# Block product 5 of the K and V projections by seven smaller products

## The chip, the cores and the metric

The kernel runs on one core of a Trainium2 chip. The metric is the device time of one execution in microseconds (us), taken as the median of several runs; lower is better. Engines are named as in the profile: PE is TensorE (matrix products), PEld its weight loads, DVE is VectorE, ACT is ScalarE, POOL is GpSimd, SP is SyncE, which here only issues DMAs.

## The reference

A cross-attention layer followed by a feed-forward layer, in float32. There are 8 batches of 128 queries and 128 keys, a width of 512, 32 heads of 128, and a feed-forward width of 1376.

```python
x = x + xattn(layernorm(x), ctx, mask)      # xattn adds its own residual, and has an RMS norm first
  h_q = rmsnorm(h) @ w_q.T ; h_k = ctx @ w_k.T ; h_v = ctx @ w_v.T      # 512 -> 32 heads x 128
  score = softmax(where(mask, h_q h_k^T + position_bias, -inf))
  out = (score @ h_v) @ w_out.T
x = x + (silu(x' @ Wg.T * ag) * (x' @ Wu.T * au)) @ Wd.T * ad           # x' = layernorm(x)
```

## The kernel before

**Seven products for eight.** Each large matrix product is cut into 2 x 2 blocks and computed with the seven products of Strassen's scheme in Winograd's form instead of eight. For a projection, the weights give the blocks a11, a12, a21, a22 and the sums s1, s2, s4 (`combine_rows`, `sums_a`, on GpSimd; a21 is overwritten), the context tokens give the other factor (`ctx_t`). Numbered 1 to 7 the products add up to four output parts: product 1 goes to all, 6 to all but (1,1), 7 to (2,2) and (2,1), 5 to (2,2) and (1,2), while 2, 3 and 4 go to one part each: (1,1), (1,2) and (2,1).

**Two levels.** Of the 14 key and value projections of groups 1 to 7 (a group is four heads), eleven are "parted": the values of group 1 (v1), and keys and values of groups 2 to 6 (k2 to v6). There, products 1, 6, 7 and 5 are made as large tiles (`four`: two tiles for each product, banks "mm", copied out by ACT in L379, product 5 added to its two parts by VectorE in L377). Products 2, 3 and 4, the block products with a single target, are each split once more into 2 x 2 blocks and made by seven smaller products (`inner`, `inner_T` for keys, `inner_V` for values). `inner` takes seven steps. A step multiplies one of the seven small products for all three blocks, into a pair of banks ("one" or "two"), and VectorE adds what comes out to the output (L401). The banks accumulate over the steps: small products 1, 6, 7, 4 use the pair "one" and 2, 5, 3 the pair "two", in the order 2, 1, 6, 7, 4, 5, 3.

The smaller products need sums of their own. `inner_rows` makes them of the weights on GpSimd: one set of four additions over blocks 2 and 4 together (256 elements each), one set over block 3 (128 elements). `inner_tokens` makes them once of the tokens: for blocks 2 and 3 at the start, for block 4 in four additions that `ctx_later` hands out to VectorE one by one, one for each of the batches 0 to 3 of group 0.

**The order of the work.** `later_kv` is a generator that emits a projection's large tiles and, behind them, single steps of the projection's `inner`, one tile and one step in turn; the last five steps lie among the tiles of the next projection. It also calls `begin` (the next projection's `combine_rows`) and `inner_rows` at certain tiles k. The attention runs over groups g and batches b: `probabilities` (scores `sc` in L512, added to the masked bias in L516, row maximum, four exponentials in L525, row sums in L532, division L536), `transpose_p` (a VectorE transpose L273, a DMA `turned` to memory and a DMA `pT` back, L275 and L280), and `attend` (`av`, L558), which runs three batches later. After each batch, products are drawn from `later_kv` until their units (`FULL` for a tile, `PART` for a step) reach `due(g, b)`; so the projections of group g+1 fill TensorE between the batches of group g.

Engines wrapped in `InOrder` keep the program's order: TensorE, VectorE and ACT up to batch 3 of group 0, GpSimd up to the end of group 1. Everything else is ordered ahead of time by the framework's planner, which goes by the order of the program and its own estimate of times, and may bring later work forward.

The pool `ipool` holds the token sums (one tile for each inner block) and the row sums; `spool` holds s1, s2, s4 and `wpool` the weights, with three buffers each.

Of the kernel before, what the change touches and what calls it, by code (L numbers as in the profile page):

```python
# [10 lines left out]
F32 = mybir.dt.float32  # L11
# [6 lines left out]
P = 128  # L18
# [16 lines left out]
class Later:  # L35
# [10 lines left out]
    def next(self, engine):  # L46
        if self.calls:
            op, args, kw = self.calls.pop(0)
            getattr(engine, op)(*args, **kw)
# [15 lines left out]
def xattn_ffn_kernel(  # L65
# [32 lines left out]
    HC = DC // 2  # L98
    HW = GW // 2
# [15 lines left out]
    proj, rows, attn, wts = ExitStack(), ExitStack(), ExitStack(), ExitStack()  # L115
# [183 lines left out]
    def sums_a(eng, a11, a12, a21, a22, s1, s2, s4):  # L299

        eng.tensor_tensor(s1, a21, a22, ADD)
        eng.tensor_tensor(s2, s1, a11, SUB)
        eng.tensor_tensor(a21, a11, a21, SUB)
        eng.tensor_tensor(s4, a12, s2, SUB)
        return {1: a11, 2: a12, 3: s4, 4: a22, 5: s1, 6: s2, 7: a21}
# [9 lines left out]
    def combine_rows(name, w):  # L315

        a11, a12 = w[:, :HC, :HW], w[:, HC:, :HW]
        a21, a22 = w[:, :HC, HW:], w[:, HC:, HW:]
        s = spool.tile([P, 3, HC, HW], F32, tag="S", name=f"S_{name}")
        s1, s2, s4 = s[:, 0], s[:, 1], s[:, 2]  # L320
        rows = sums_a(gpsimd, a11, a12, a21, a22, s1, s2, s4)
        rows["lower"] = w[:, HC:]
        return rows

    def token_sums(eng3, eng4, b11, b12, b21, b22, t1, t2, t4):
# [57 lines left out]


    SINGLE = (2, 3, 4)

    def inner(name, multiply, places, banks=None, order=(2, 1, 6, 7, 4, 5, 3)):

# [15 lines left out]
    def inner_T(name, a, b, heads):  # L404
# [8 lines left out]

        return inner(name, multiply, (((2, 3), upper), ((4,), lower)))

    def inner_V(name, a, b, pairs):
        def multiply(n, i, out, first):
            for k in range(2):
                kv_tensor.matmul(  # L419
                    out[:, bass.ts(k, S)], b[n][i][:, bass.ts(k, S)], a[n][i],  # L420
                    start=first and k == 0, stop=True, skip_group_check=True,
                )

        def left(r, c, m):
            to = pairs[c - 1].rearrange("p k (h n) -> p h k n", h=2)[:, :, :, bass.ts(r - 1, P)]
            return [(to, m.rearrange("p h (k n) -> p h k n", k=2))]

        def right(r, c, m):
            to = pairs[c + 1][:, :, bass.ts(r - 1, P)]
            return [(to, m[:, 0].rearrange("p (k n) -> p k n", k=2))]  # L430

        return inner(name, multiply, (((2, 4), left), ((3,), right)))

    def numbered(b11, b12, b21, b22, t1, t2, t3, t4):
        return {1: b11, 2: b21, 3: b22, 4: t4, 5: t1, 6: t2, 7: t3}
# [161 lines left out]

    FULL, PART, FIRST = 4, 3, 3.8  # L600

    def later_kv():


        def place(n):
            t = ipool.tile([P, 4, HW], F32, tag=f"t{n}", name=f"t_c{n}")
            return (t[:, k] for k in range(4))

        def inner_rows(name, w):

            s = ipool.tile([P, 3, 3, P], F32, tag="rows", name=f"s_{name}", bufs=2)
            lower = w["lower"].rearrange("p c (n r q) -> p c n r q", n=2, r=2)
            both = [lower[:, c, :, r] for r in range(2) for c in range(2)]
            three = [w[3][:, c, bass.ts(r, P)] for r in range(2) for c in range(2)]
            sums = sums_a(gpsimd, *both, *(s[:, k, :2] for k in range(3)))
            a = {n: {i: rows[:, k] for i, rows in sums.items()} for k, n in enumerate((2, 4))}
            a[3] = sums_a(gpsimd, *three, *(s[:, k, 2] for k in range(3)))
            return a

        todo = [(g, kind) for g in range(1, NG) for kind in "kv"]  # L620
        made, rows = {}, {}

        def begin(n):

            g, kind = todo[n]
            if g not in made:
                made[g] = dict(zip("kv", kv_w.pop(g)))
            rows[n] = combine_rows(f"{kind}{g}", made[g].pop(kind))

        begin(0)  # L630
        b, steps = inner_tokens(vector, ctx_t, HW, place, (2, 3)), iter(())
        b.update(inner_tokens(ctx_later, ctx_t, HW, place, (4,)))
        for n, (g, kind) in enumerate(todo):
            name, w = f"{kind}{g}", rows.pop(n)
            out = kvs.setdefault(g, ([], []))["kv".index(kind)]
            parted = 0 < n and g + 1 < NG
            if parted:
                blocks, smaller = (blocks_T, inner_T) if kind == "k" else (blocks_V, inner_V)
                tiles = four(name, *blocks(name, w, ctx_t, out))
            else:  # L640
                tiles = (project_T if kind == "k" else project_V)(name, w, ctx_t, out)
            for k in itertools.count():

                if k == 5 and n + 1 < len(todo):
                    begin(n + 1)
                if k == 2 and parted:
                    a = inner_rows(name, w)
                if next(tiles, "none") == "none":
                    break
                yield FULL if n else FIRST  # L650
                if k == 6 and parted:
                    steps = smaller(name, a, b, out)
                if next(steps, None):
                    yield PART

# [8 lines left out]
    kv_tensor = InOrder(tc, nc.tensor)  # L664
# [26 lines left out]
    for n, _ in enumerate(first_kv()):  # L691
        if n in moments_at:
            pair[moments_at[n]] = norm1_moments(moments_at[n])
        if n in scales_at:
            b = scales_at[n]
# [182 lines left out]
    def due(g, b):  # L878


        tiles, steps = 2 * 8 * FULL, 2 * 7 * PART
        late = 5 * PART
        if g == 0 and b < 4:
            return (5 + 3 * b) * FIRST
        if g < NG - 2:
            start = 14 * FULL if g == 0 else g * (tiles + steps) - late
            end, n, k = (g + 1) * (tiles + steps) - late, 4 if g == 0 else B, b - 4 if g == 0 else b
        else:
            start, n, k = g * (tiles + steps) - late, B, b
            end = start + late + 25 * FULL  # L890
        return start + (end - start) * (k + 1) / n - 1.5
# [5 lines left out]
    for g in range(NG):  # L897
# [21 lines left out]
        for b in range(B):  # L919
# [14 lines left out]
            if g == NG - 1:  # L934


                if b + 2 < B:
                    biased.append(masked_bias(gpsimd, g, b + 2, pb))
                for _ in range(2):
                    wo_later.next(gpsimd)  # L940
                if wo_sums:
                    wo_sums = wo_sums(gpsimd)

                def between():
                    if b == 0:
                        next(products)
                    fetched[b] = att_sums(b, 0, come.pop((b, 0)), vector)

                p = probabilities(g, b, qT, kT, pb, between, biased.pop(0))
            elif g == 0 and b < 4:  # L950
                def one():
                    nonlocal done
                    done += next(products)

                def one_and_sum():
                    ctx_later.next(vector)
                    one()

                if b == 0:
                    biased = [masked_bias(gpsimd, g, k, pb) for k in range(2)]  # L960
                biased.append(masked_bias(gpsimd, g, b + 2, pb))
                p = probabilities(g, b, qT, kT, pb, one_and_sum, biased.pop(0), one)
            elif g == 0 and b < 6:
                p = probabilities(g, b, qT, kT, pb, s=biased.pop(0))
            else:
                p = probabilities(g, b, qT, kT, pb)
                if g == NG - 2:
                    for _ in range((0, 1, 1, 1, 1, 2, 2, 2)[b]):
                        wo_later.next(InOrder(tc, nc.gpsimd))
# [299 lines left out]
    def inner_F(i, a, outs):  # L1269
        def multiply(n, k, out, first):  # L1270
            nc.tensor.matmul(  # L1271
                out, a[n][k], fine_t[n][k], start=first, stop=True, skip_group_check=True
            )


        def both(k, r, c, m):
            to = outs[k][r - 1].rearrange("p (c n) -> p c n", c=2)[:, :, bass.ts(c - 1, HW)]
            return to, m

        def upper(r, c, m):  # L1280
            return [both(0, r, c, m)]

        def lower(r, c, m):
            to, _ = both(0, r, c, m)
            return [both(1, r, c, m), (to[:, 1], m[:, 1])]

        pl = ps.pools[1]
        banks = [
            pl.tile([P, 2, HW], F32, tag=tag, name=f"i_{i}_{k}", bufs=bufs)
            for k, (tag, bufs) in enumerate(3 * [("m", 3)] + [("tp", 1)])  # L1290
        ]
        return inner(
            f"f{i}", multiply, (((2, 3), upper), ((4, 5), lower)), (banks[:2], banks[2:]),
            (2, 1, 5, 6, 3, 7, 4),
        )

    gpsimd = nc.gpsimd
# [203 lines left out]
```

## Time and profile before

| | us |
|---|---|
| median of 3 runs | 1074.88 (1074.33 to 1076.42) |
| the profiled execution | 1076.96 |
| its span | 1075.2 |
| mean granted TensorE clock | 0.998 of full |
| TensorE busy | 1066.8 |
| VectorE busy | 675.3 |
| GpSimd busy | 489.8 |
| ACT busy | 332.5 |

The profile is of one execution. Its time is 1.76 us longer than its span, and 2.08 us longer than the median of the runs. Attention of group 0 begins at about 242 us, group 0's batches end near 291 us, and each of the groups 1 to 5 then takes 60.3 us. The parted projections lie from 269 to 617 us. Lines are named L401 and so on; a line can be that of a helper (L60 is `InOrder`). In rows of groups, the name left of the arrow is what is written, then come partitions x elements, the count, the busy time in us, the mean of one in ns, and idle time of the engine before it.

### The profile page before, as it was taken

How to read it: one execution, taken by the hardware profiler on the slowest of the kernel's cores; microseconds unless marked ns; L12 is line 12 of the kernel's file. 1: busy time of each engine (PE TensorE's matmuls, PEld its weight loads, DVE VectorE, ACT ScalarE, POOL GpSimd, SP SyncE). 2: the span in 40 equal slices, each digit the busy share in tenths (PEclk: the TensorE clock that was granted, in tenths of full speed). 3: DMA queues.
4: the chain of work that ended last, by engine and by line, in shares of the span. 5: the costliest groups of instructions: out<-in, count | busy, mean ns of one | idle time of the engine just before them, and what ended most of it. 6: DMA issues, size and time to landing. Idle time of an engine off the chain costs nothing.

```text
span 1075.2 us, 14043 instructions
## 1 busy us (share of the span) xinstructions
PE 1066.8 (99%) x4904; PEld 811.3 (75%) x4904; DVE 675.3 (63%) x1232; ACT 332.5 (31%) x902; POOL 489.8 (46%) x543
## 2 busy tenths in 40 slices
PE   9999999999999999999999999999999999999998
PEld 5656666655878888887978769998888875666887
DVE  4653443447757777777777766894454338889852
ACT  2633323214444444444444334221000012333100
POOL 6233455525655455555553373662000337897010
PEclk9999999999999999999999999999999999999999
DMA  9613344545665455464555566873542532110011
GB/s 291 196 57 118 117 152 166 192 165 198 196 206 184 160 164 183 157 211 165 198 187 187 169 213 214 274 235 125 190 138 78 171 124 59 40 41 18 1 40 40
DMA packets 124693, 161.82 MB, mean 151 GB/s; under 512 B 15600, under 2 KB 77296, under 8 KB 124624
## 3 DMA queue, kind: packets, MB, share of 16 engines
q1 hardware_dynamic: 110208, 129.73, 36.5%
q10 hardware_dynamic: 12544, 24.38, 6.5%
q0 software_dynamic: 1872, 6.82, 2.0%
q8 instruction: 39, 0.64, 0.2%
q14 instruction: 30, 0.25, 0.1%
HBM read 104.81 MB, written 56.10 MB: 150 GB/s over the span
## 4 chain that ended last, share of the span: by engine, by line
PE 93%; DMA 3%; DVE 2%; ACT 1%; issue 1%; ACTq 0%; POOL 0%; SPq 0%; DVEq 0%; POOLq 0%
PE mm_q L458 10%; PE m L843 9%; PE mm_k L458 9%; PE mm_v L479 9%; PE m L60 7%; PE d L1407 6%; PE i_q L406 6%; PE i L1271 6%; PE i_v L419 5%; PE mm_f L1312 5%; PE i_k L406 4%; PE av L558 4%; PE sc L512 4%; PE mm_k L60 3%; PE mm_v L60 2%; PE mm_q L60 1%
## 5 line engine op out<-in xcount | busy, mean ns | idle before, releaser
L497 POOL TENSOR_TENSOR s<-pb,mneg 128x512 f32<-128x512 f32 x40 | 61.3, 1533 | 112.1 <-DVE p L536 86.3
L401 DVE TENSOR_TENSOR q<-q,i_q 128x512 f32<-128x512 f32 x98 | 49.9, 550 | 82.2 <-PE i_q L406 82.0
L525 ACT ACTIVATE s<-s,nmx 128x128 f32<-128x128 f32 x240 | 93.4, 390 | 23.3 <-DVE nmx L60 11.7
L563 ACT COPY aT<-av 128x512 f32<-128x512 f32 x60 | 35.1, 586 | 162.6 <-PE av L558 130.3
L60 POOL TENSOR_TENSOR s<-pb,mneg 128x512 f32<-128x512 f32 x24 | 36.7, 1533 | 79.2 <-DVE p L60 39.6
L379 ACT COPY q<-mm_q 128x512 f32<-128x512 f32 x56 | 31.5, 588 | 94.9 <-PE mm_q L458 67.7
L512 PEld LDWEIGHTS sc<-k,q 128*128 128x128 f32 x416 | 54.1, 192 | 8.2 <-issue 5.3
L458 PE MATMUL mm_q<-hT,wq 128*128 128x512 f32 x128 | 58.5, 592 | 0.0
L479 PE MATMUL mm_v<-wv,ctx_sb 128*128 128x256 f32 x248 | 58.0, 379 | 0.0
L60 POOL TENSOR_TENSOR S_q<-wq 128x512 f32<-128x512 f32 x8 | 10.1, 1268 | 104.2 <-ACT wq L60 104.2
L558 PE MATMUL av<-pT,v 128*128 128x128 f32 x416 | 55.0, 275 | 2.2 <-DMA pT<-turned 2.2
L479 PE MATMUL mm_v<-S_v,ctx_sb 128*128 128x256 f32 x240 | 56.4, 379 | 0.0
L458 PE MATMUL mm_q<-hT,S_q 128*128 128x512 f32 x120 | 55.9, 592 | 0.0
L512 PE MATMUL sc<-k,q 128*128 128x128 f32 x416 | 55.3, 275 | 0.0
L516 DVE TENSOR_TENSOR s<-sc,s 128x512 f32<-128x512 f32 x52 | 35.7, 686 | 30.2 <-PE sc L512 29.4
L458 PE MATMUL mm_k<-ctx_sb,wk 128*128 128x512 f32 x112 | 54.1, 608 | 0.0
L401 DVE TENSOR_TENSOR v<-v,i_v 128x512 f32<-128x512 f32 (+1 forms) x84 | 43.5, 540 | 15.3 <-PE i_v L419 15.3
L558 PEld LDWEIGHTS av<-pT,v 128*128 128x128 f32 x416 | 50.6, 192 | 2.4 <-issue 2.4
L479 PEld LDWEIGHTS mm_v<-wv,ctx_sb 128*128 128x128 f32 x248 | 46.3, 190 | 5.8
L60 PE MATMUL m<-wo,a 128*128 128x256 f32 x200 | 48.5, 380 | 0.8 <-DMA a<-att 0.8
L458 PE MATMUL mm_k<-ctx_sb,S_k 128*128 128x512 f32 x104 | 48.6, 593 | 0.0
L843 PE MATMUL m<-wo,a 128*128 128x256 f32 x200 | 48.4, 379 | 0.0
(374 smaller groups left out, 2559.8 us busy)
## 6 DMA issues: line engine op xcount, KB each, us to landing
queries<-q SPq DMA_DIRECT2D x32, 512.0 KB, 3.9
turned<-tt SPq DMA_DIRECT2D x64, 256.0 KB, 2.8
pT<-turned SPq DMA_DIRECT2D x64, 256.0 KB, 3.0
att<-aT ACTq DMA_DIRECT2D x64, 256.0 KB, 3.1
q<-queries SPq DMA_DIRECT2D x30, 512.0 KB, 6.0
a<-att SPq DMA_DIRECT2D x23, 512.0 KB, 4.1
wq<-in_wqT_dram SPq DMA_DIRECT2D x8, 1024.0 KB, 6.6
wk<-in_wkT_dram SPq DMA_DIRECT2D x7, 1024.0 KB, 5.4
```

Source lines behind the costliest of these rows:

```text
L60: return self.tc.keep_in_program_order(getattr(self.engine, op)(*args, **kw))
L401: vector.tensor_tensor(to, to, out, ADD)
L406: kv_tensor.matmul(out, a[n][i], b[n][i], start=first, stop=True, skip_group_check=True)
L458: kv_tensor.matmul(out, w[i][:, c, bass.ts(t, P)], src[i][:, c, :], start=(first and c == 0), stop=(c == HC - 1), skip_group_check=True,)
L479: kv_tensor.matmul(out[:, bass.ts(k, HW)], src[i][:, c, bass.ts(2 * t + k, S)], w[i][:, c, :], start=(first and k == 0 and c == 0), stop=( ...
L497: eng.tensor_tensor(s.rearrange("q h (j r) -> q h j r", r=BS), pb.rearrange("q h (r j) -> q h j r", r=BS), mneg[:, b : b + 1, :].rearrange ...
L512: tensor.matmul(sc[:, j, :], qT[:, j, bass.ts(b % 2, S)], kT[j][:, cols], start=True, stop=True)
L525: scalar.activation(s[:, j, :], s[:, j, :], AF.Exp, bias=nmx[:, j : j + 1], accum_out=sm[:, j : j + 1],)
L558: tensor.matmul(av[:, j, :], v[b // 2][:, b % 2, bass.ts(j, P)], pT[:, :, j, :], start=True, stop=True,)
L843: tensor.matmul(m[n], sa[n][:, c, :], wo_t[g][n][:, c, :], start=(g == order[0] and c == 0 and PRODUCTS.index(n) % 2 == 0), stop=(g == ord ...
L1271: nc.tensor.matmul(out, a[n][k], fine_t[n][k], start=first, stop=True, skip_group_check=True)
L1407: nc.tensor.matmul(out, lhs, rhs, start=bank not in started, stop=(i == NP - 1 or n == 8), skip_group_check=True,)
```

## The change

In the eleven parted projections, product 5 is no longer made as two large tiles. It becomes a fourth inner block: `four` is called with `fifth=False`, and `inner_T5` (for keys) and the changed `inner_V` multiply blocks 2, 3, 4 and 5 in each step. Block 5 shares the second bank with block 4 (keys) or 3 (values), and VectorE reads that bank twice in a step: once the whole of it (512 elements), and once block 5's half (256), which goes to its second part.

The order of the small products becomes `ALTERNATE` = 2, 1, 5, 6, 3, 7, 4, which the feed-forward layer used already under no name. `inner_rows` works on blocks 5 and 3 together, as on 2 and 4, from s1 and s4. `inner_tokens` gets four additions more, for block 5, which batches 4 and 5 of group 0 hand to VectorE, two each, between their exponentials and row sums.

A projection now has six tiles and seven steps; two steps follow the sixth tile, and the other five lie among the next projection's tiles. `begin` for the next projection is called at tile 3 instead of 5, `inner_rows` at 1 instead of 2. `PART` is 4 instead of 3, and `due` counts 6 tiles for 8.

```diff
-        rows["lower"] = w[:, HC:]
+        rows["lower"], rows["sums"] = w[:, HC:], s
...
+    ALTERNATE = (2, 1, 5, 6, 3, 7, 4)
...
+    def inner_T5(name, a, b, heads):
+        def multiply(n, i, out, first):
+            kv_tensor.matmul(out, a[n][i], b[n][i], start=first, stop=True, skip_group_check=True)
+
+        def both(head, c, m):
+            return head.rearrange("p (c n) -> p c n", c=2)[:, :, bass.ts(c - 1, HW)], m
+
+        def upper(r, c, m):
+            return [both(heads[r - 1], c, m)]
+
+        def lower(r, c, m):
+            to, _ = both(heads[r - 1], c, m)
+            return [both(heads[r + 1], c, m), (to[:, 1], m[:, 1])]
+
+        return inner(name, multiply, (((2, 3), upper), ((4, 5), lower)), order=ALTERNATE)
...
         def right(r, c, m):
-            to = pairs[c + 1][:, :, bass.ts(r - 1, P)]
-            return [(to, m[:, 0].rearrange("p (k n) -> p k n", k=2))]
-
-        return inner(name, multiply, (((2, 4), left), ((3,), right)))
+            to = pairs[c + 1].rearrange("p k (h n) -> p h k n", h=2)[:, :, :, bass.ts(r - 1, P)]
+            m = m.rearrange("p h (k n) -> p h k n", k=2)
+            return [(to, m), (to[:, 0], m[:, 1])]
+
+        return inner(name, multiply, (((2, 4), left), ((3, 5), right)), order=ALTERNATE)
...
-    FULL, PART, FIRST = 4, 3, 3.8
+    FULL, PART, FIRST = 4, 4, 3.8
...
-            s = ipool.tile([P, 3, 3, P], F32, tag="rows", name=f"s_{name}", bufs=2)
+            s = ipool.tile([P, 3, 4, P], F32, tag="rows", name=f"s_{name}", bufs=2)
             lower = w["lower"].rearrange("p c (n r q) -> p c n r q", n=2, r=2)
-            both = [lower[:, c, :, r] for r in range(2) for c in range(2)]
-            three = [w[3][:, c, bass.ts(r, P)] for r in range(2) for c in range(2)]
-            sums = sums_a(gpsimd, *both, *(s[:, k, :2] for k in range(3)))
-            a = {n: {i: rows[:, k] for i, rows in sums.items()} for k, n in enumerate((2, 4))}
-            a[3] = sums_a(gpsimd, *three, *(s[:, k, 2] for k in range(3)))
+            outer = w["sums"][:, 0:3:2].rearrange("p n c (r q) -> p c n r q", r=2)
+            a = {}
+            for k, (names, rows) in enumerate((((2, 4), lower), ((5, 3), outer))):
+                sums = sums_a(
+                    gpsimd, *(rows[:, c, :, r] for r in range(2) for c in range(2)),
+                    *(s[:, i, bass.ts(k, 2)] for i in range(3)),
+                )
+                for j, n in enumerate(names):
+                    a[n] = {i: row[:, j] for i, row in sums.items()}
             return a
...
-        b.update(inner_tokens(ctx_later, ctx_t, HW, place, (4,)))
+        b.update(inner_tokens(ctx_later, ctx_t, HW, place, (4, 5)))
...
-                blocks, smaller = (blocks_T, inner_T) if kind == "k" else (blocks_V, inner_V)
-                tiles = four(name, *blocks(name, w, ctx_t, out))
+                blocks, smaller = (blocks_T, inner_T5) if kind == "k" else (blocks_V, inner_V)
+                tiles = four(name, *blocks(name, w, ctx_t, out), fifth=False)
...
-                if k == 5 and n + 1 < len(todo):
+                if k == (3 if parted else 5) and n + 1 < len(todo):
                     begin(n + 1)
-                if k == 2 and parted:
+                if k == 1 and parted:
                     a = inner_rows(name, w)
...
-                if k == 6 and parted:
+                if k == 5 and parted:
                     steps = smaller(name, a, b, out)
+                    next(steps)
+                    yield PART
...
-        tiles, steps = 2 * 8 * FULL, 2 * 7 * PART
+        tiles, steps = 2 * 6 * FULL, 2 * 7 * PART
...
             elif g == 0 and b < 6:
-                p = probabilities(g, b, qT, kT, pb, s=biased.pop(0))
+                def two_sums():
+                    for _ in range(2):
+                        ctx_later.next(vector)
+
+                p = probabilities(g, b, qT, kT, pb, two_sums, biased.pop(0))
```

More of the change, by code (lines that the diff above doesn't have):

```diff
@@ L1293, in inner_F @@
             f"f{i}", multiply, (((2, 3), upper), ((4, 5), lower)), (banks[:2], banks[2:]),
-            (2, 1, 5, 6, 3, 7, 4),
+            ALTERNATE,
         )
```

## The prediction

> **What bounds the kernel now.** I read the page first, then what TensorE waits for, then the busy time by stretch of the stage that the change touches, then the chain of work in time order there.
>
> ```profile
> PE 1066.8 (99%) x4904; PEld 811.3 (75%) x4904; DVE 675.3 (63%) x1232; ACT 332.5 (31%) x902; POOL 489.8 (46%) x543
> PE av L558 <- DMA pT<-turned: 2.2, 1, 2.2
> core 0: us, PE busy (x) PEld busy (x) DVE busy (x) ACT busy (x) POOL busy (x), PEclk, DMA share, GB/s
> 357.00:417.00 60.00, 60.00 (x350) 49.62 (x349) 44.75 (x85) 26.40 (x88) 32.52 (x33) 1.00 0.55 180
> 295.00:299.50 4.50, 4.50 (x16) 2.50 (x15) 0.53 (x1) 2.82 (x10) 4.42 (x4) 0.62 0.64 196
> ```
>
> TensorE is busy for 99% of the span and in 357 to 417 us, one head group of the steady stage, for all of it. VectorE has 15 us free there and GpSimd 27, so what counts is the number of matrix columns, unless another engine becomes late. Between 239 and 669 us TensorE waits once: 2.2 us, for a transposed probability block coming back from memory. After it the clock falls to half.
>
> ```profile
> 284.84 6.17 DMA turned<-tt
> 291.03 3.34 DMA pT<-turned
> 294.50 1.13 PE av L558 x8
> 295.63 3.25 PE mm_k L458 x4
> 298.88 1.50 PE i_v L419 x12
> ...
> 389.51 1.29 PE i_k L406 x6
> 390.80 1.73 PE mm_v L479 x8
> ...
> 416.11 0.89 PE sc L512 x8
> 417.00 0.89 PE av L558 x8
> 417.89 1.72 PE mm_k L458 x4
> 419.61 1.34 PE i_v L419 x12
> ```
>
> These are start, length, work. Each record is one of the two passes of a float32 matmul, so "mm_k x4" is one large tile (two matmuls of 512 columns, 1.72 us), "mm_v x8" one of V (1.73), "i_k x6" one small step for three block products (1.29), "i_v x12" the same for V (1.34). Large and small columns cost alike: 1.29/6 = 0.215 us per 256 columns (K), 1.34/12 = 0.112 per 128 (V). The V steps are 3% dearer per column than mm_v (1.73/8 = 0.216 per 256).
>
> **Change on TensorE.** Each of 11 projections (v1, and keys and values of groups 2 to 6) loses the two tiles of product 5 and gains a fourth block in seven steps.
> K: 2 x 1.72 = 3.44 goes, 7 x 2 records x 0.215 = 3.01 comes: -0.43. V: 2 x 1.73 = 3.46 goes, 7 x 4 x 0.112 = 3.13 comes: -0.33. Five of K and six of V: -2.15 - 1.98 = -4.1 us, all on the path, as TensorE has no gap there to swallow it. Scores, `av` and the last projections (k7, v7) keep their work.
>
> **VectorE.** It gets the wider and the extra addition (names, shape, count, busy, mean ns):
>
> ```profile
> L401 DVE TENSOR_TENSOR v<-v,i_v 128x512 f32<-128x512 f32 x42 | 28.3, 673 | 15.3 <-PE i_v L419 15.3
> L401 DVE TENSOR_TENSOR v<-v,i_v 128x256 f32<-128x256 f32 x42 | 17.1, 406 | 0.0
> L377 DVE TENSOR_TENSOR v<-v,mm_v 128x512 f32<-128x512 f32 x24 | 15.6, 670 | 6.3 <-PE mm_v L479 6.3
> ```
>
> Per projection four L377 additions go (4 x 0.67 = 2.7 us), seven of 256 become 512 (7 x 0.27 = 1.9) and seven of 256 are new (7 x 0.41 = 2.8): +2.0 us, +4.1 per group. The stretch rises from 44.75 of 60 to about 48.8 of 59.5, 82%. I cost it at nothing: its cover is the free time, and the banks. A step must wait until VectorE has read the bank that it refills. In the old order 2,1,6,7,4,5,3 the steps 1,6,7,4 use one pair of banks in a row, and TensorE waits for none of them. In 2,1,5,6,3,7,4 only 7 and 4 follow each other, a tile of 1.72 us between them. Since the upper pair is written first (0.9 us), the lower bank has 2.6 us; its two additions need 1.08. If softmax work (L536, 0.93 us on average here, and L273, 0.71) stands in front of them, that is 2.7: about at the edge, so the bound is from 0 to some 0.6 us per projection. I take 0, the nearest row being the four tight successions now.
>
> **GpSimd.** `inner_rows` makes eight additions of 256 instead of four of 256 and four of 128: in 357 to 477 us these take 0.73 and 0.46, so +4 x 0.27 = 1.1 us per projection. It comes a tile earlier, and the four sums of `combine_rows` (1.27 us each) two tiles earlier. Neither issues a DMA; the weights were asked for a group before. In group 0 `S_k` (5.1 us) moves ahead of the masked bias of batch 6: that bias ran at 269.7 and would run near 276, while its scores are ready only near 280. The bias of batch 7 began at 277.4 on a VectorE release, so it stays. Later, `S_v` made at 404.8 us is first used near 456. Nothing.
>
> **The four more token sums** on VectorE (0.42 us each, the same t_c rows near 240 us) fall between the exponentials and the row sums of batches 4 and 5, where VectorE idles 1.72 us before L532. Nothing; if the cover were gone, 0.84 us per batch.
>
> **Pacing, and the one stall.** This is where I expect gain to go. Steady groups go from 106 to 104 units, about 13 per batch in both, and an `av` comes three batches after its scores, some 21 us, against about 14 for scores at 400.2 to `pT` asked for at 410.8 plus 3 us: safe. But in group 0 the batches 5 to 7 get less work between them. By `due`, before the `av` that stalls TensorE does 8 tiles of v1 and two steps: 8 x 1.73 + 2 x 1.34 = 16.5 us. After the change it does 6 tiles and two steps of 1.79: 14.0. So it reaches that `av` 2.5 us earlier. The block it waits for hangs on other things: a bias load that SyncE issues at 278.98 once GpSimd has read the old one, behind it `turned` (279.39), `pT` (283.21), a query load (283.62), `turned` (284.84, 6.17 us to land) and `pT` (291.03). All of that follows batch 4's softmax, which the change does not move. What waits behind that `av` is all of TensorE's queue, and ACT's copy. So the block lands near 294.5 as before, and the idle time grows from 2.2 to about 4.8 us: +2.5. Bounds: -4.0 if the stall goes (2.25 idle, and 1.53 + 0.16 lost to the half clock in the rows at 295.63 and 298.88), +3.2 if scores of batch 6, arriving 1.7 us sooner, also put a 0.7 us addition ahead of batch 5's row sums. I take +2.5, since the chain of loads is the row that ends last.
>
> The row shows a clock of 0.62 in 295.0 to 299.5 after only 2.2 us idle, so I count the clock loss as paid in both kernels. The Trainium skill, "TensorE: Matmul & The Clock Gate", Part 1, says that the clock halves after an idle window of about 3.4 us and recovers after one busy window. Read strictly, the short gap should not have halved it and the longer one would: an estimate of 1.7 us more, which would make the net +0.1. The trace already contradicts that reading.
>
> **Sum.** -4.1 + 2.5 = -1.6 us. The profiled execution took 1076.96 us (1.76 around its 1075.2 us span); it would take 1075.4. The median of the plain runs is 1074.88, 2.1 lower; I carry the difference over: 1073.3. That lies within 0.2% of before (2.15 us), about the least that a measurement of this kernel tells from no change.
>
> **Rivals.**
> *The stall does not grow (chance 0.33).* TensorE's order there is planned, not fixed by hand: the trace runs 16 small V records already at 243.4 us, ahead of most of k1, and splits scores at 626.1. If the planner sees the gap it can put k2's first tile (1.72 us) before the `av`; its banks are now freed by ACT's copies, not by the VectorE additions of product 5. One tile leaves -4.1 + 0.8 = -3.3; idle unchanged -4.1 (1070.8); a tile and a step could end the stall and the clock loss: -8.0 (1066.9). Against it: it put this `av` directly after the scores before. I price the case at -4.1.
> *VectorE becomes late (chance 0.16; slower).* The place is the lower bank between steps 7 and 4. It decides from 0.33 us per projection on: 11 x 0.33 = 3.7 us turns -1.6 into +2.1. At 0.6 each it is +6.6 - 1.6 = +5.0: 1079.9. For it: 82% busy, two steps in one 7.0 us batch need 3.44 + 3.5 = 6.9 us of VectorE, and single L536 rows of 1.7 us occur. Against: no bank wait now, and two steps' distance between most uses of a bank.
> *The query load goes ahead of `turned` (chance 0.06).* It adds its own 2 us or so of transfer to the stall: about +0.5, no change.
>
> **How the numbers follow.** The growing stall has 0.45: 1073.3, own range 1072.5 to 1074.5. The 80% range reaches down to 1068.8 (a stall mostly gone) and up to 1077.5 (a VectorE delay of 0.35 us or so): about 0.08 lies below and 0.11 above. Faster by over 0.2% takes the rival of 0.33 and some 0.06 of the first case, 0.39; slower takes 0.17; no change 0.44.
>
> **What would show it.** Right: i_k x8 at 1.72 and i_v x16 at 1.79 between tiles; six tiles per projection; a group of 59.5 us instead of 60.3; VectorE near 48.8 us in it; one TensorE wait on `pT` in group 0, near 4.8 us, ending near 294.5. Wrong: `i` matmuls waiting for L401 additions in the steady stage, a wait on `pT` of 2 us or none, or a second one.

## The result, and the profile after

The changed kernel takes 1079.56 us (1078.91 to 1080.23, five runs) against 1074.88 us of before (five runs): 1.0038 times as long, 95% interval 1.0021 to 1.0055. It is slower by 4.7 us where 1.6 us less was forecast. The profiled execution took 1080.23 us with a span of 1078.1 us (before: 1076.96 and 1075.2), so profile against profile it is +3.3 us.

The page's busy times:

```profile
PE 1063.7 (99%) x5006; PEld 817.7 (76%) x5006; DVE 683.0 (63%) x1269; ACT 331.1 (31%) x902; POOL 497.2 (46%) x543
```

What TensorE waits for (in total, times, longest):

```profile
PE av L576 <- DMA pT<-turned: 5.5, 2, 4.9
PE m L60 <- DMA a<-att: 1.5, 1, 1.5
PE mm_k L476 <- DVE k L364: 1.3, 1, 1.3
...
PE m L60 <- POOL wo L60: 0.3, 1, 0.3
```

The busy time by stretch, a steady group and the time behind the stall (columns as shown for before):

```profile
357.00:417.00 60.00, 60.00 (x375) 51.58 (x374) 47.61 (x91) 26.17 (x88) 35.85 (x34) 1.00 0.56 181
...
296.16:300.50 4.34, 4.34 (x14) 3.02 (x15) 0.00 (x0) 1.85 (x8) 4.26 (x5) 0.64 0.49 144
```

TensorE is 3.1 us less busy and the kernel is longer, so the loss is waiting. The steady stretch is as forecast: no wait, VectorE at 47.61 of 60. The wait on `pT` in group 0 has grown from 2.2 us to 5.5, and the clock behind it is again at 0.64. Three waits lie near the end of the projections and behind them: TensorE waits 1.3 us for k7's additions (L364), the attention output `att` 1.5 (before 0.8), the output projection's weight sums 0.3.

The chain of work in time order, around the stall and in a steady group (start, length, work):

```profile
286.32 6.75 DMA turned<-tt
...
293.09 2.94 DMA pT<-turned
...
296.16 2.05 PE av L576 x8
298.21 2.32 PE mm_k L476 x4
...
388.21 1.73 PE mm_v L497 x8
389.94 1.73 PE i_k L419 x8
```

The `av` that waited starts at 296.16 instead of 294.50. It and the next tile take 2.05 and 2.32 us instead of 0.89 and 1.72: 1.76 us lost to the restart at the lower clock. The K step is "i_k x8" at 1.73, as forecast.

### The profile page after: what moved, and what is told of

The parts are those of the page before. It is cut to its first block, busy times and chain, and to the rows that moved or that the text cites. A ratio compares the mean times of both kernels' runs of the same rounds, so it can differ in the third digit from the quotient of the medians.

```text
span 1078.1 us, 14312 instructions
## 1 busy us (share of the span) xinstructions
PE 1063.7 (99%) x5006; PEld 817.7 (76%) x5006; DVE 683.0 (63%) x1269; ACT 331.1 (31%) x902; POOL 497.2 (46%) x543
## 4 chain that ended last, share of the span: by engine, by line
PE 91%; DMA 4%; DVE 2%; issue 1%; POOL 0%; ACT 0%; SPq 0%; ACTq 0%; DVEq 0%; POOLq 0%
PE mm_q L476 10%; PE m L867 9%; PE mm_v L497 8%; PE i_v L436 7%; PE mm_k L476 7%; PE d L1435 6%; PE i_q L407 6%; PE i L1299 6%; PE i_k L419 6%; PE m L60 5%; PE mm_f L1340 5%; PE av L576 4%; PE sc L530 4%; PE mm_k L60 3%; PE mm_v L60 2%; PE mm_q L60 1%
## 5 line engine op out<-in xcount | busy, mean ns | idle before, releaser
L402 DVE TENSOR_TENSOR q<-q,i_q 128x512 f32<-128x512 f32 x98 | 49.9, 550 | 82.2 <-PE i_q L407 82.0
L402 DVE TENSOR_TENSOR v<-v,i_v 128x512 f32<-128x512 f32 (+1 forms) x126 | 73.6, 588 | 30.3 <-PE i_v L436 18.7
L402 DVE TENSOR_TENSOR k<-k,i_k 128x512 f32<-128x512 f32 (+1 forms) x105 | 60.1, 588 | 27.8 <-PE i_k L419 27.2
L301 DVE TENSOR_TENSOR S_a<-a 128x256 f32<-128x256 f32 x22 | 9.6, 434 | 58.8 <-DMA a<-att 34.1
L1074 POOL TENSOR_TENSOR x<-x,u 128x256 f32<-128x256 f32 x4 | 3.0, 752 | 91.3 <-DVE x L1073 91.3
```

The costliest lines, as they stand in the source:

```text
L402: vector.tensor_tensor(to, to, out, ADD)
```

## The theories

**W (waits).** The matrix saving is there, and waits elsewhere take back more than it: the shorter fill in group 0, the half clock behind it, and GpSimd's work that comes at other times.
**V (load).** The eleven projections themselves became dearer: VectorE's 4 us per group and the new order of the small products, spread over the steady groups.

One number explains the fill. `due` gives the batches 4 to 7 of group 0 what lies between 14 tiles (56 units) and a group's total less `late`. Before: 64 + 42 - 15 - 56 = 35 units. After: 48 + 56 - 20 - 56 = 28, as `late` is `5 * PART` and `PART` went from 3 to 4. The experiments on the fill change this number, in either kernel.

## Experiments on the fill

**The changed kernel with 12 units more drawn in group 0** (40 instead of 28).

```diff
-        late = 5 * PART
+        late = 5 * PART - 12
```

> The changed kernel with one number altered: the projections are drawn 12 units (three tiles or steps, 5.2 us of TensorE) earlier in every group. The work is the same. Theory W (waits): the change saves its matrix work as reckoned, and loses it in a few local waits, the largest of them the two waits of 0.7 and 4.9 us on pT in group 0. Then these vanish or fall under 1 us in all, the clock stays full there, and the time falls by 5 to 7 us against the changed kernel, to about 1073.5. Theory V (VectorE and GpSimd load): the extra additions slow the whole stage, wherever the tiles lie. Then the time falls by no more than 1 us.

1071.02 us (1070.53 to 1072.57), against 1076.16 of before on this chip: 0.9952 (0.994 to 0.9965). The wait in group 0 is gone, the mean clock is 1.0 in each of the five runs. These are its waits of 0.9 us and more:

```profile
PE m L60 <- DMA a<-att: 1.3, 1, 1.3
PE zero L177 <- DVE zeros L174: 1.2, 1, 1.2
PE mm_v L497 <- DVE k L364: 0.9, 1, 0.9
```

One constant is worth some 8.5 us here (1079.56 to 1071.02, on different chips; by the ratios 0.86%, 9 us). V is out as the main cause: the same work on every engine is now faster than before. It is more than the 5 to 7 us that were expected, and more than the stall and the clock together (5.5 + 1.8); the wait on L364, too, is shorter by 0.4.

**The kernel before with the same edit** (47 units instead of 35), to see what the edit gives without the change.

> The kernel before with its projections drawn 12 units earlier, as a control: what its own single wait of 2.2 us is worth. Theory W: the wait goes, and with it the half clock behind it: 2.2 to 3.9 us below the kernel before, 1071.0 to 1072.7. With the run of both alterations this gives the change's worth without waits: 4.1 us less matrix work. Theory V: the kernel with both alterations is slower than this one by 3 us or more.

1072.65 us (1072.51 to 1074.11), 0.9969 (0.9957 to 0.9981), no wait on `pT`, clock 1.0 in all five runs. So the edit gives 3.5 us before and 8.5 after, and between the two kernels without the stall the change is worth 1.6 us, not 4.1. Their traces differ by more: from the first scores to the output projection's first matmul it is 422.90 us (242.49 to 665.39) here and 420.56 (243.15 to 663.71) in the changed kernel with 12 units, 2.3 us less. The rest lies where the two kernels do the same.

**The changed kernel with the old order of the small products** (2, 1, 6, 7, 4, 5, 3), first alone, then with the 12 units.

```diff
-        return inner(name, multiply, (((2, 3), upper), ((4, 5), lower)), order=ALTERNATE)
+        return inner(name, multiply, (((2, 3), upper), ((4, 5), lower)))
```

(and the same in `inner_V`)

> The changed kernel with the small products of the key and value projections in the old order 2, 1, 6, 7, 4, 5, 3. Theory W: the new order puts the two small products that read the weights' lower half (7 and 4) last, so each weight buffer comes free two steps later; the load of wo2 (609.3 us before, 616.8 after) returns to about 610, GpSimd's sums behind it too, and the 1.3 us wait of the k7 tile near 636 us goes. The group 0 waits stay. Time 1.5 to 2.8 us below the changed kernel. Theory V: the order that reuses one bank pair four times in a row makes TensorE wait for the wider additions in the steady stage; the groups grow past 59.6 us and the time doesn't fall.

> Both alterations. Theory W: no wait on pT in group 0, none at the k7 tile, groups of 59.5 us: 7 to 9 us below the changed kernel, 1070.5 to 1072.5, and under the kernel before. Theory V: within 1 us of the changed kernel.

Alone: 1080.04 us (1078.4 to 1083.97), 1.004 (1.0026 to 1.0054). With 12 units: 1071.7 us (1071.02 to 1073.09), 0.9961 (0.9949 to 0.9973). Neither differs measurably from the new order. With the old order the weights' lower half is read for the last time earlier, and the load of `wo` that the changed kernel issues at 616.79 us goes out at 613.21; the k7 wait disappears; but steps wait for VectorE instead (i_v on L402, 0.6 to 0.7 us). So what I had ascribed to the order (1.5 to 2.8 us) does not show in the time.

**The kernel before with the changed kernel's short fill** (29 units). No work is changed.

```diff
-        late = 5 * PART
+        late = 5 * PART + 6
```

> The kernel before, with the products in front of the late batches drawn 6 units later (a tile and a step), so that its group 0 has as short a fill as the changed kernel's. No work is changed. Theory W: the wait on pT grows from 2.2 to about 5.3 us, the half clock is paid in every run; +3.1 us, and up to +4.9 where the kernel before did not pay the clock: 1078.5 to 1081. Theory V: the work is the same, so within 1 us of the kernel before.

1081.3 us (1080.52 to 1083.07) against 1075.13: 1.0051 (1.0033 to 1.0068), clock 0.997 to 0.998 in all eight runs. The line of TensorE where it waits:

```profile
294.60 1.13 PE L558 MATMUL av<-pT,v 128*128 128x128 f32 x8 [4.19 <-DMA pT<-turned]
```

The short fill alone makes the kernel before slower by 6 us, more than the whole change does. The wait on `pT` is 4.4 us in all, less than the 5.3 expected, and the time lies a little above the expected range; not all of the 6 us is assigned. And the block of probabilities lands where it did in before (294.60 against 294.50), though both query loads are issued ahead of `turned` here as in the changed kernel. So the order of these loads alone is not what brought the changed kernel's block 1.66 us later.

**The changed kernel with 8 units more** (36, one more than before had).

> The changed kernel with the products in front of the late batches drawn 8 units ahead (two tiles) instead of 0; 12 units gave 1071.0. Theory W, as a dose: two tiles are 3.4 us of work moved in front of the stalled av, so 1.5 to 2.1 us of the wait of 5.5 are left; time -3.4 us against the changed kernel in the wait, and a further -1.7 where the short wait no longer costs the half clock: 1074.4 to 1076. Theory V: the draw changes nothing, about 1079.6.

1070.89 us (1069.47 to 1075.59), 0.9957 (0.9939 to 0.9976). The wait on `pT` is 0.6 us, less than the 1.5 to 2.1 expected, since the block also lands earlier: `pT` is asked for at 290.96 instead of 293.09. The time lies 3.5 us below the expected 1074.4 to 1076, and cannot be told from 12 units.

What differs is seen on SyncE, which issues the loads. The first line is the changed kernel's, the second that of 8 units:

```profile
284.76 1.47 SPq L899 DMA_DIRECT2D q<-queries  x2
```

```profile
284.47 0.85 SPq L899 DMA_DIRECT2D q<-queries  x1
```

With 8 units only one query load is issued ahead of `turned`, as in before, and the block lands 51.27 us behind the first scores (242.78 to 294.05). In before it is 52.00, in the changed kernel 53.21.

## Experiments on what GpSimd delays

The block of probabilities goes through batch 4's softmax. In the changed kernel its division (L554) takes 1.78 us instead of 0.69 (L536). In before the masked bias of batch 6 was long done by then. The two records are:

```profile
276.56 0.69 DVE L536 TENSOR_TENSOR p<-s,ri 128x512 f32<-128x512 f32 x1
```

```profile
269.74 1.52 POOL L60 TENSOR_TENSOR s<-pb,mneg 128x512 f32<-128x512 f32 x1
```

In the changed kernel, first VectorE's, then GpSimd's records around it, in the order in which they run:

```profile
275.82 0.51 DVE L550 TENSOR_TENSOR ri<-sm,unseen 128x4 f32<-128x4 f32 x1 [1.72 <-ACT s L543]
276.37 0.18 DVE L551 RECIPROCAL ri<-ri 128x4 f32<-128x4 f32 x1
276.58 1.78 DVE L554 TENSOR_TENSOR p<-s,ri 128x512 f32<-128x512 f32 x1
```

```profile
275.05 1.26 POOL L60 TENSOR_TENSOR S_k<-wk,S_k 128x512 f32<-128x512 f32 x1
276.27 1.54 POOL L60 TENSOR_TENSOR s<-pb,mneg 128x512 f32<-128x512 f32 x1
```

GpSimd's masked bias of batch 6 ends at 276.27 + 1.54 = 277.81, and the division at 276.58 + 1.78 = 278.36, 0.55 later: it looks as if it could do nothing while GpSimd ran. The small `ri` before it, 128 x 4 elements, takes 0.51 us and ends at 276.33, as `S_k` does (276.31). The Trainium skill, "SBUF — State Buffer", section "SBUF: two separate sides", states that the port pair which GpSimd and VectorE share is an exclusive lock held for a whole instruction, also when a VectorE instruction has two SBUF inputs and the GpSimd instruction reads SBUF. Both hold for the division and the bias, and these rows agree with it.

**The changed kernel with k2's row sums asked for at tile 5 again**, so that they come behind the bias of batch 6, as before.

```diff
-                if k == (3 if parted else 5) and n + 1 < len(todo):
+                if k == (3 if n > 1 and parted else 5) and n + 1 < len(todo):
```

> The changed kernel with k2's row sums asked for at tile 5 again in group 0, so that GpSimd makes S_k of k2 behind the masked bias of batch 6 instead of ahead of it; everything else as changed. Theory W (waits: the short fill in group 0 makes the stall, and GpSimd's earlier sums push the block itself later): batch 4's division L536/L554 falls from 1.78 to about 0.7 us, the pT block lands about 1.1 us earlier (near 295.0 instead of 296.1 us), the wait is 3.5 to 4.4 instead of 4.9 us, the half clock behind it stays, time -0.5 to -1.5 us against the changed kernel, so about 1078 to 1079 on a chip where that one takes 1079.6. If the earlier sums are not what moves the block: it lands at 296 again, time unchanged. Theory V (VectorE's added load, spread over all projections, makes the loss): unchanged within 0.5 us.

1079.81 us (1077.61 to 1081.76, twelve runs), 1.0035 (1.002 to 1.0049). The expectation on the division failed: it took 1.51 us, now beside `S_k` (276.18 to 277.46), which had moved into the bias's place. The block landed 0.95 us earlier than in the changed kernel, 0.35 of that from an earlier start of the attention. The time did not move. The reason was read off its GpSimd records: the sums of `inner_rows` in front, four of them 0.72 to 1.17 us instead of 0.45 to 0.90 each, hold the chain up by 1.1 us, wherever the bias stands.

**The same, and for v1 the sums over blocks 5 and 3 made 128 elements wide, as before.**

```diff
+                j0 = k if name == "v1" else 0
                 sums = sums_a(
-                    gpsimd, *(rows[:, c, :, r] for r in range(2) for c in range(2)),
-                    *(s[:, i, bass.ts(k, 2)] for i in range(3)),
+                    gpsimd, *(rows[:, c, j0:, r] for r in range(2) for c in range(2)),
+                    *(s[:, i, 2 * k + j0 : 2 * k + 2] for i in range(3)),
                 )
                 for j, n in enumerate(names):
-                    a[n] = {i: row[:, j] for i, row in sums.items()}
+                    a[n] = {i: row[:, max(j - j0, 0)] for i, row in sums.items()}
```

> The changed kernel with GpSimd's load around batch 4's division brought back to that of before: k2's row sums asked for at tile 5 again in group 0, and for v1 alone the set of sums over blocks 5 and 3 made 128 elements wide instead of 256 (block 5's small products of v1 are made from block 3's sums, so the values of group 1 come out other than the reference's). With k2's sums moved alone the division still took 1.51 us and the block landed 0.95 us earlier. Theory W with GpSimd as the cause of the late block: S_k ends near 276.3 us, the division takes 0.7 to 0.9 us, the block lands near 294.6, the wait is 3.5 to 3.9 us, time -0.5 to -1.2 us against the changed kernel. If the division is slow for another reason (the new order on VectorE): 1.5 us or more again, and the block at 295.2 or later.

The division is back, and the wait is shorter; VectorE's and TensorE's records:

```profile
276.94 0.69 DVE L554 TENSOR_TENSOR p<-s,ri 128x512 f32<-128x512 f32 x1
```

```profile
295.10 2.04 PE L576 MATMUL av<-pT,v 128*128 128x128 f32 x8 [4.18 <-DMA pT<-turned]
```

The block lands at 295.10, 52.22 us behind the first scores (242.88); in the changed kernel it was 53.21, in before 52.00. So with GpSimd's sums as before 1.0 us of the block's delay goes, from one profile of each kernel. It is not GpSimd alone: with 8 units the division takes 1.78 us as well, and the block is not late.

```profile
276.43 1.78 DVE L554 TENSOR_TENSOR p<-s,ri 128x512 f32<-128x512 f32 x1
```

Two query loads ahead of `turned` and a fast division (before with the short fill) give 52.21 us, one load and a slow division (8 units) 51.27. The block is later than that only where both come together, as in the changed kernel. How they add up was not tried by itself. In time it is 1079.44 us (1077.9 to 1080.8), 1.0025 times (1.0014 to 1.0035) the 1076.7 that before took on this chip. Against the changed kernel's 1.0038 the sign is as expected, but the intervals overlap. The wait came out 0.3 us above the upper bound of its expectation.

**The second place is k7.** In the last stretch of the projections TensorE waits for an addition (L364) that stands behind a division, and that division stands beside GpSimd (TensorE's, VectorE's, then GpSimd's records of the changed kernel):

```profile
636.28 1.98 PE L476 MATMUL mm_k<-ctx_sb,S_k 128*128 128x512 f32 x4 [1.32 <-DVE k L364]
```

```profile
633.15 1.76 DVE L554 TENSOR_TENSOR p<-s,ri 128x512 f32<-128x512 f32 x1
...
635.58 1.25 DVE L364 TENSOR_TENSOR k<-k,mm_k 128x512 f32<-128x512 f32 x2
```

```profile
632.83 1.52 POOL L515 TENSOR_TENSOR s<-pb,mneg 128x512 f32<-128x512 f32 x1
```

Again the division ends (634.91) 0.56 us behind GpSimd's instruction (634.35). GpSimd reaches this bias only now, as sums of `S_v` and the output projection's sums `T_o` stand in front of it. The first of these `T_o` waited 4.55 us for its load of `wo` and began at 622.57 us; with the old order, where the k7 wait is gone, it began at 618.67.

**The changed kernel with 12 units and `T_o` handed to GpSimd later**, none with batches 0 to 2, two each from batch 3 on.

```diff
-                    for _ in range((0, 1, 1, 1, 1, 2, 2, 2)[b]):
+                    for _ in range((0, 0, 0, 2, 2, 2, 2, 2)[b]):
```

> The changed kernel, drawn 12 units ahead (1071.0), and in the last parted groups GpSimd is handed the output projection's sums T_o later: none with batches 0 to 2, two each with batches 3 to 7, so that the values' row sums S_v come ahead of them and no GpSimd sum lies beside the division that k7 or v7 waits for. Theory W: the 0.9 us wait of mm_v on L364 and the 0.4 to 0.6 us of small waits around v7 go; 1070.0 to 1071.0. If the sums then finish too late for the output projection: a wait of m on wo L60 above 0.3 us, and no gain.

1069.99 us (1069.18 to 1072.81) against 1075.13 of before on its chip: 0.9944 (0.9923 to 0.9965). The wait on L364 falls from 0.9 to 0.4 us. The small waits that the expectation places around v7 are not there: the one of 0.4 us lies at 52.57 us, ahead of the attention, the one of 0.2 us in v1 (282.79), and that one stays. **The kernel before with both edits** is its counterpart:

> The kernel before, drawn 12 units ahead and with the output projection's sums handed to GpSimd late: the counterpart of the best version of the changed kernel, which took 1069.99 against 1075.13 of before. Matrix work says that the changed kernel saves 4.1 us on it. Theory W, in which the change's own worth is 4.1 us less what new waits take back: 1072.5 to 1074 here, 3 to 4 us above the changed kernel with both edits. If the late sums help before too by 1 us: 1071.6, and the change itself is worth only 1.6.

1072.83 us (1072.71 to 1074.85), 0.9972 (0.9961 to 0.9983): in before the later sums bring nothing (0.9969 without). The ratio of the two, 0.9944 / 0.9972, makes the change worth 0.28%, 3.0 us; the two intervals just overlap. Their traces agree: from the first scores to the output projection's first matmul it is 422.90 us in before's version (242.82 to 665.72) and 420.00 in the changed one's (244.08 to 664.08).

**8 units and the later sums together.**

> The changed kernel drawn 8 units ahead and with the output projection's sums late. 8 units alone gave 1070.9, 12 units with the late sums 1070.0. Theory W: a wait of about 0.6 us on pT in group 0, no wait on L364; 1069.5 to 1071. Expected equal to the version with 12 units within 1 us.

1072.45 us (1070.06 to 1072.74), 0.9957 (0.9944 to 0.997), with a wait of 0.9 us on `pT` and none on L364. The median is above the range that was expected, on a chip where before takes 1076.7. By their ratios the four versions (8 or 12 units, with or without the later sums) are not to be told apart, and each beats both kernels. Against the kernel before with the same edits the change is worth 1.6 to 3.0 us at 12 units: it pays, by less than the forecast, once group 0 is filled again. With 8 units and the later sums it is 0.4 us below the kernel before with both edits (1072.45 against 1072.83, on one chip).

## Why the prediction was wrong, step by step

**Matrix work, -4.1: right.** A steady group takes 59.55 us instead of 60.28, as forecast. Between the stalled `av` and v7's first tile 343.75 us became 343.73, and the sum of the steps gives nearly that: five K and five V at -0.43 and -0.33 (-3.8), the five steps of v1 that come behind the stall at +0.45 each (+2.25), k7's wait (+1.32) and the restart behind it (1.98 instead of 1.72): +0.03.

**The stall, +2.5: right in kind, too small.** It grew by 3.3 us (2.25 to 5.55, both waits on `pT`; a second wait was among the signs of being wrong). The planner put no tile into the gap, so the rival at 0.33 did not occur. The fill gave 2.1 of the 3.3, a little less than the 2.5 forecast. The step "the block lands near 294.5 as before" failed: it landed at 296.16, 1.21 us later against the first scores. With GpSimd's sums as before 1.0 of that is gone. That the query loads go ahead of `turned`, a rival at 0.06, did happen; in before with the short fill they did so too, and the block landed at 294.60. In the changed kernel `turned` took 6.75 us to land instead of 6.17. The records fit a block that is late where the late division and the second query load come together, but how the 1.21 us divide between the two stays open.

**"GpSimd. Nothing": wrong.** The prediction had the row: the bias of batch 6 "ran at 269.7 and would run near 276". It ran at 276.27. It asked only when that bias's own scores were ready, and not which VectorE instruction would lie beside it: batch 4's division, at 276.56 in before. With it fell the premise that the change does not move batch 4's softmax. The division took 1.1 us longer, and up to 1.0 us of the block's delay hangs on it. The wait at k7, where a division stands beside GpSimd again, is another 1.3.

**"I count the clock loss as paid in both kernels": wrong, and the largest single term.** The profiled execution of before had paid it. Its plain runs mostly had not, if their mean clock is read so: of 48 runs of before beside the experiments 18 show a mean clock of 0.997 or 0.998, and 30 show 0.999 or 1.0. The medians of the spans, paid against not paid, are 1075.9 and 1073.9, 1075.4 and 1073.0, 1075.3 and 1073.85 us on the three chips: 1.5 to 2.4 us. The kernels whose profiled execution waits 4 us or more show the lower clock in every run: five of five of the changed kernel, 35 of 35 of its variants and of before with the short fill. So I put +1.7 to the medians, an estimate from the profile of before (1.53 + 0.16). How long the wait was in the executions without a profile is not known. The rule of the Trainium skill, "TensorE: Matmul & The Clock Gate", Part 1 (an idle window of about 3.4 us halves the clock), which the prediction weighed and set aside by one profiled row, would have made the net +0.1. The runs agree with it for the long wait; behind the short one the clock fell in some executions only.

**VectorE, 0: right.** No wait in the steady groups, 47.61 us of 60 (48.8 of 59.5 forecast). That rival, with 0.16 for slower, did not occur; the kernel became slower by the case that was forecast, a stall that grows, with two terms that the forecast had set at nothing.

**Not in the sum:** the stretch from the output projection's first matmul to its wait on `att` is 1.3 us longer (86.92 to 88.25), with 0.6 of that in the wait and 0.3 in the wait on the weight sums; the first scores start 0.45 us later. Neither was tried by itself. The start varied from 242.39 to 244.36 us among kernels that are equal there, and the stretch to `att` from 86.80 to 89.21 us among the 13 traces, so both terms are within what single profiles differ by.

In the two profiles the terms add up along TensorE's path: the start +0.45, the block +1.21, from there to v7 -0.02, to the output projection's first matmul 0.00 (31.32 us in both), to `att` +1.33, behind it -0.07: +2.9, the difference of the spans. With 1.7 for the clock that is 4.6 for the medians, against 4.7 measured. In the prediction's terms it is -4.1 + 3.3 + 1.7 + 1.3 + 1.3 + 0.45 = +3.95; what is missing there is the fill, which shrank by 2.1 us where the steps give 2.56, and the restart at k7.

Why the versions without a stall gain 3.0 us or less instead of 4.1 is only in part known: with 12 units and the later sums 0.6 us of it are two waits, 0.4 on L364 in front of v7 and 0.2 in v1.

## What to carry to other kernels

A saving on the engine that is the bound is worth what its thinnest stage lets through: when work gets smaller, recount what every wait was filled with, above all where a pacing constant is derived from a cost that the change alters (`5 * PART`). When an instruction moves on GpSimd, look up which VectorE instruction will run beside it. And before a loss is booked as "paid in both", look at several executions: the one that was profiled need not be the usual one.

## What the runs showed of the hardware

The mean clock of plain runs, set beside the wait on `pT` in the one profiled execution of the same kernel: with a wait of 2.2 us 18 of 48 runs show 0.997 or 0.998 and the others 0.999 or 1.0; with 0.6 or 0.9 us it is 6 of 14; without a wait on `pT` 2 of 28; with 4 us and more all 40 of 40 show 0.998 or less. In the profile of before the clock was 0.62 in the 4.5 us behind the wait of 2.2 us.

A VectorE instruction with two SBUF inputs ended 0.54 to 0.56 us behind the end of the GpSimd instruction beside it, at three places (1.51 to 1.78 us instead of 0.69), and one of four elements per row took 0.51 us instead of 0.16, probably for the same reason. None of these was measured by itself.
